# Paged attention on one core: block transposes on VectorE and transfers within SBUF in place of TensorE transposes

## The chip, the cores and the metric

One core of a Trainium2 chip runs the whole kernel. The metric is device time in microseconds (us) of one execution. Less is better.

## The reference, cut to what matters

The input x has 64 sequences of 32 tokens of 512 numbers. First each sequence is multiplied by a small matrix chosen by its condition and added to itself. Then follows attention over a paged cache of keys and values with new keys appended. All of it is float32.

```python
x = x + einsum('bct,bcd->bdt', x, weights[condition])
q = einsum('bsd,ed->bse', x, Wq).reshape(64, 32, 32, 128)     # 32 query heads
k = einsum('bsd,ed->bse', x, Wk).reshape(64, 32, 8, 128)      # 8 key heads
v = einsum('bsd,ed->bse', x, Wv).reshape(64, 32, 8, 128)
q, k = rope(rmsnorm(q, q_norm_w), pos), rope(rmsnorm(k, k_norm_w), pos)
k_all = concat([k_cache[block_table] (512 rows), k]); v_all likewise
scores = einsum('bqhd,bkhd->bhqk', q, repeat(k_all, 4)) * SCALE   # 4 query heads share a key head
probs = softmax(where(valid, scores, -1e30))
o = einsum('bhqk,bkhd->bqhd', probs, repeat(v_all, 4))
out = x + einsum('bse,de->bsd', o.reshape(64, 32, 4096), Wo)
```

## The kernel before, in words

A **step** handles 4 sequences (128 tokens, one per partition) and 4 of the 8 key heads with their 16 query heads. There are 32 steps: 16 groups of sequences for the first half of the heads (`hh` 0), then the same 16 for the second half (`hh` 1). The output of the first half waits in DRAM in `acc_d`, and the transposed input of a group in `x1t_d`.

Each step is cut into 16 **slots**, one for each sequence (`bt`) and key head (`g`); slot = 4 bt + g. A slot always has the scores of one head against 512 cached keys (`ps`, L534), the exponential on ScalarE (`pr`, L542) and the product of probabilities and values of the slot before (`po`, L592). Around these, the loop issues by a table the preparation of the *next* step, called `ahead`:

- `x1_c` (`pmix`, L353) and `x1_b` (`px1t`, L361) mix and transpose the input, in slots 2 and 3, for steps of the first half only;
- `k_a` and `q_a` project (`pp`, L397: 8 TensorE instructions with 512 columns), then `norm_rope` normalises and rotates on ScalarE, VectorE and GpSimd: `sq` L407, `ms` L411 and L412, `rs` L414, `rope` and `ropeu` L418, L425, L431, L433;
- `k_b` and `q_b` transpose the 128x128 result of each of four heads on TensorE (`pt`, L441) and copy it out of PSUM on ScalarE (L454, L469). There are five such groups of four in a step, in slots 6, 8, 10 and 13;
- `v_a` projects the new values.

`out_proj` of the step *before* (`pout`, L481, 32 TensorE instructions) stands whole in slot 3. The scores against new keys (`psn`, L552) are in slot 0, their values (`pnv`, L576, copied out at L584) in slots 1 and 3. `psn`, `pnv`, `pp`, `pt`, `pmix`, `px1t` and `pout` share a ring of four PSUM tiles.

The keys of a sequence come as 16 transfers of 64 KB from the SP queue (`k_t`, L286), issued in the first slot of a sequence for the sequence after the next one. They land in one of two buffers, and VectorE copies them head by head into one of four `kh` tiles (L527). Values come by indirect transfers from GpSimd (`raw`, L310, three buffers) and are masked by ScalarE (`v`, L323). `turn` (L617) is a VectorE transpose in 32x32 blocks, used here for the attention output alone. TensorE's and SP's instructions run in the order in which the program writes them; the order on the other engines is a scheduler's.

Of the kernel before, what the change touches and what calls it, by code (L numbers as in the profile page):

```python
# [19 lines left out]
P = 128  # L20
# [35 lines left out]
def cond_resid_paged_attention_kernel(  # L56
# [67 lines left out]
    rden = const.tile([P, NHH * NT * BT, GH], F32, tag="rden", name="rden")  # L124
# [61 lines left out]
    def steps_of(exact, pools):  # L186
# [31 lines left out]

        last = {}
# [44 lines left out]

        def load_x(t):
            xt = work.tile([P, HID], F32, tag="acc", name=f"xt_{t}_{uid}", bufs=3)
            nc.sync.dma_start(xt, x[t * P : (t + 1) * P, :])
            return xt
# [62 lines left out]
        class Step:  # L331
            def __init__(self, n):
                self.n, self.hh, self.t = n, n // NT, n % NT
                self.name = f"{n}_{uid}"
                self.qt = {}

        def x1_a(st):

            nonlocal x_next
            t = st.t  # L340
            if st.hh:
                st.acc = work.tile([P, HID], F32, tag="acc", name=f"acc_{st.name}", bufs=3)
                nc.sync.dma_start(st.acc, acc_d[t])
                st.x1t = work.tile([P, KC, P], F32, tag="x1t", name=f"x1t_{st.name}", bufs=1)
                nc.sync.dma_start(st.x1t.rearrange("p c q -> p (c q)"), x1t_d[t])
                return
            st.acc = x_next
# [54 lines left out]
        def norm_rope(st, pp, name, kind):  # L402

            cw, sw = st.rot[kind]
            p4 = pp.rearrange("p (h e f) -> p h e f", h=4, e=2)
            sq = work.tile([P, 4, D], F32, tag="w2", name=f"sq_{name}", bufs=1)
            nc.scalar.activation(  # L407
                sq.rearrange("p h d -> p (h d)"), pp, AF.Square, scale=1.0 / math.sqrt(D)
            )
            ms = small.tile([P, 4], F32, tag="ms", name=f"ms_{name}")  # L410
            nc.vector.tensor_reduce(ms, sq, AX.X, ALU.add)  # L411
            nc.vector.tensor_scalar_add(ms, ms, EPS)  # L412
            rs = small.tile([P, 4], F32, tag="rs", name=f"rs_{name}")
            nc.gpsimd.tensor_tensor(rs, ms, minus_half, ALU.pow)  # L414

            r = work.tile([P, 4, 2, HD], F32, tag="w1", name=f"rope_{name}")
            u = work.tile([P, 4, 2, HD], F32, tag="w2", name=f"ropeu_{name}", bufs=1)
            nc.vector.tensor_tensor(  # L418
                r.rearrange("p h e f -> p h (e f)"),
                pp.rearrange("p (h d) -> p h d", h=4),  # L420
                cw.rearrange("p e f -> p (e f)").unsqueeze(1).to_broadcast([P, 4, D]),
                ALU.mult,
            )
            for e in range(2):
                nc.vector.tensor_tensor(  # L425
                    u[:, :, e, :],
                    p4[:, :, 1 - e, :],
                    sw[:, e, :].unsqueeze(1).to_broadcast([P, 4, HD]),
                    ALU.mult,
                )  # L430
            nc.vector.tensor_tensor(r, r, u, ALU.add)  # L431
            rd = r.rearrange("p h e f -> p h (e f)")
            nc.vector.tensor_tensor(  # L433
                rd, rd, rs.unsqueeze(2).to_broadcast([P, 4, D]), ALU.mult
            )
            return rd
# [6 lines left out]

        def k_a(st):
            if st.n > 1 or exact:
                rot_tables(st)
            name = f"k_{st.name}"
            pp = project(st, wt["k", st.hh, 0], f"pp_{name}")
            st.k_rope = norm_rope(st, pp, name, "k")

        def k_b(st):
            pt = transposed(st.k_rope, f"k_{st.name}")
            st.kn = act.tile([P, GH, P], F32, tag="kn", name=f"kn_{st.name}")
            nc.scalar.copy(st.kn, pt)  # L454
# [6 lines left out]
        def q_a(st, g):  # L461
            name = f"q_{st.name}_{g}"
            pp = project(st, wt["q", st.hh, g], f"pp_{name}")
            st.qt[g] = norm_rope(st, pp, name, "q")

        def q_b(st, g):
            pt = transposed(st.qt[g], f"q_{st.name}_{g}")
            qt = act.tile([P, BT, REP, S], F32, tag=f"qt{g}", name=f"qt_{st.name}_{g}")
            nc.scalar.copy(  # L469
                qt.rearrange("p b h s -> p h b s"),  # L470
                pt.rearrange("p h (b s) -> p h b s", b=BT),
            )
            st.qt[g] = qt

        def out_proj(st, halfway=None):

            po = ps_p.tile([P, HID], F32, tag="pp", name=f"pout_{st.name}")
            for i in range(QH):
                if halfway and i == 3 * QH // 4:
                    halfway()  # L480
                nc.tensor.matmul(  # L481
                    po,
# [5 lines left out]
            nc.vector.tensor_tensor(st.acc, po, st.acc, ALU.add)  # L488
            if exact or st is steps[-1]:
                store(st)  # L490
# [27 lines left out]
        def queries(ba, g):  # L518
            return ba.st.qt[g][:, ba.bt].rearrange("p h s -> p (h s)")
# [25 lines left out]
        def new_scores(st):  # L545
# [3 lines left out]
            for g in range(GH):  # L549
                for bt in range(BT):  # L550
# [3 lines left out]
                        st.kn[:, g, own],  # L554
                        st.qt[g][:, bt].rearrange("p h s -> p (h s)"),
# [30 lines left out]
        def values(ba, g):  # L586
# [12 lines left out]
            if g == 0:  # L599
                ba.o = work.tile([P, GH, D], F32, tag="o", name=f"o_{ba.name}", bufs=1)  # L600
            if g % 2:
# [3 lines left out]
                rd = rden[:, ba.n, both]  # L605
# [17 lines left out]
        def exact_batch(ba, key_no):  # L623
# [7 lines left out]
            for g in range(GH):  # L631
# [9 lines left out]
                    st.kn[:, g, bt * S : (bt + 1) * S],  # L641
# [43 lines left out]
        x_next = load_x(0)  # L685
        if exact:
# [7 lines left out]
            for st in steps:  # L694
# [6 lines left out]
                if st.n:  # L701
                    x_next = st.hh or load_x(st.t)
                if not st.hh:
                    load_cond_weights(st.t)
                x1_a(st)
                x1_c(st)
                x1_b(st)
                k_a(st)
# [8 lines left out]
                out_proj(st)  # L717
# [3 lines left out]
        first, second = steps[0:2]  # L721
        load_w("q", 0, 0)
# [15 lines left out]
        x_second = load_x(1)  # L738
# [14 lines left out]
        trig = work.tile([P, 3, TRIG * HD], F32, tag="w1", name="trig0")  # L753
# [4 lines left out]
        x1_a(first)  # L758
        x1_c(first)
        x_next = x_second  # L760
# [8 lines left out]
        trig = work.tile([P, 3, TRIG * HD], F32, tag="w1", name="trig1")  # L769
# [21 lines left out]
        x1_a(second)  # L791
# [30 lines left out]
        def pieces(st):  # L822
            do = {
                0: (x1_a,),
                4: (k_a, (q_a, 0)),
                5: ((q_a, 1),),
                6: (v_a, k_b, (q_b, 0)),
                8: ((q_a, 2), (q_b, 1)),
                10: ((q_a, 3), (q_b, 2)),
                13: ((q_b, 3),),  # L830
            }
            if st is second:
                do[4], do[6] = ((q_a, 0),), (k_b, (q_b, 0))
            return do

        valued, turned = (batch, GH - 1), batch
# [13 lines left out]
        x_next = load_x(2)  # L850
        load_cond_weights(2)
        for st in steps:
            if st.n:
                new_ot(st)
            ahead = steps[st.n + 1] if st.n + 1 < len(steps) else None
            fill = pieces(ahead) if ahead else {}
            for bt in range(0 if st.n else 1, BT):
# [5 lines left out]
                for g in range(GH):  # L863
# [14 lines left out]
                    if slot == 2 and ahead:  # L878
                        x1_c(ahead)
                    if slot == 3:  # L880
                        if ahead:
                            x1_b(ahead)
                        out_proj(steps[st.n - 1])
                        if st.n + 1 < NT // TRIG:
                            tmp = work.tile([P, 3, TRIG * HD], F32, tag="w1", name=f"trig_{st.n}")
                            with tc.issue_after(last["dve"]), tc.issue_after(last["act"]):
                                angles((st.n + 1) * TRIG, tmp)
                    if slot == 5 and st.n:
                        store(steps[st.n - 1])
                    if slot == 6 and 0 < st.n and st.n + 2 < NT:  # L890
                        x_next = load_x(st.n + 2)
                        load_cond_weights(st.n + 2)
                    if st.t == 0:
                        load_parts([("o", i) for i in range(GH)], st.hh, slot - GH)
                    if st.n in (NT - 2, NT - 1):
                        load_parts(
                            [("k", 0), ("q", 0), ("q", 1), ("v", 0), ("q", 2), ("q", 3)],
# [3 lines left out]
                    if unfilled and (slot == GH - 1 or bt and g or unfilled[0][0] is this):  # L901
                        for _ in range(1 if bt or g == 0 else VC):
# [4 lines left out]
                    if g == 1 and turned is not None:  # L907
                        turn(turned)
                    if later is not None:
                        head_keys(later, g)  # L910
                turned = this
                batch, later = later, after
        turn(turned, slice(0, 2))
        values(*valued)
        turn(turned, slice(2, GH))


        def in_range():
            rd = rden.rearrange("p n g -> p (n g)")
            good = work.tile([P, NHH * NT * BT * GH], F32, tag="w1", name="good")  # L920
            nc.vector.tensor_scalar(good, rd, DEN_LOW, None, ALU.is_ge)
            nc.vector.scalar_tensor_tensor(good, rd, DEN_HIGH, good, ALU.is_le, ALU.mult)
            count = small.tile([P, 1], F32, tag="ms", name="count")
            nc.vector.tensor_reduce(count, good, AX.X, ALU.add)
            ones = small.tile([P, 1], F32, tag="rs", name="ones")
            nc.vector.memset(ones, 1.0)
            pc = ps_p.tile([1, 1], F32, tag="pp", name="pcount")
            nc.tensor.matmul(pc, count, ones, start=True, stop=True)
# [4 lines left out]
        out_proj(steps[-1], in_range)  # L933
# [57 lines left out]
```

## Time and profile before

| | |
|---|---|
| median of 3 runs | 2262.68 us (2262.07 to 2267.07) |
| the profiled execution's own time | 2258.59 us |
| its span in the profile | 2256.8 us |
| VectorE busy | 1076.0 us (48%) |
| ScalarE busy | 940.4 us (42%) |
| GpSimd busy | 779.8 us (35%) |
| transfers | 318.13 MB, 141 GB/s in the mean |

A busy share is an average over the whole span. TensorE instructions are pipelined, so the sum of their durations is more than the time that they take; the distance from one group's start to the next one's start tells what a group costs.

### The profile page before, as it was taken

To read this page: it belongs to the slowest core of one execution; us is meant where nothing else is said; L and a number is where in the kernel's file an instruction comes from. 1 tells how busy PE (TensorE), PEld (TensorE's weight loads), DVE (VectorE), ACT (ScalarE), POOL (GpSimd) and SP (SyncE) were. 2 spreads that over 40 slices of the span, in tenths; PEclk is the share of its full clock that TensorE was granted. 3 is DMA by queue.
4 is the path that set the end of the run, shared out by engine and by line. 5 is a ranking of instruction groups with operands and counts; after the bars stand their busy time and mean duration, and the time that the engine had idled before them with its cause. 6 is when DMAs were issued, how large, how long until landed. Compare 5 with 4: busy or idle time off the path is not lost.

```text
span 2256.8 us, 41920 instructions
## 1 busy us (share of the span) xinstructions
PE 2223.5 (99%) x13590; PEld 1565.7 (69%) x13590; DVE 1076.0 (48%) x2722; ACT 940.4 (42%) x1724; POOL 779.8 (35%) x1008
## 2 busy tenths in 40 slices
PE   8999999999999999999999999999999999999998
PEld 5767677676776677766777666777666777666775
DVE  5545455443554444543545544455444455444452
ACT  3534454444433444433444333443334443343442
POOL 4423333233433333332333333333323343233331
PEclk9999999999999999999999999999999999999999
DMA  7744544345443455435756444553344544444542
GB/s 229 195 131 128 154 134 128 114 128 154 142 121 113 130 152 155 116 113 157 229 168 169 124 137 138 154 148 115 115 145 139 160 124 127 124 130 151 159 116 74
DMA packets 364053, 318.13 MB, mean 141 GB/s; under 512 B 46800, under 2 KB 308960, under 8 KB 363824
## 3 DMA queue, kind: packets, MB, share of 16 engines
q1 hardware_dynamic: 319104, 174.44, 27.0%
q0 software_dynamic: 41712, 136.66, 20.4%
q10 hardware_dynamic: 3008, 4.25, 0.5%
q8 instruction: 110, 1.80, 0.3%
q14 instruction: 119, 0.97, 0.1%
HBM read 302.59 MB, written 12.58 MB: 140 GB/s over the span
## 4 chain that ended last, share of the span: by engine, by line
PE 90%; DMA 4%; DVE 2%; issue 2%; SPq 2%; ACT 1%; POOL 1%; ACTq 0%; DVEq 0%; POOLq 0%
PE pout_x L481 19%; PE pp_q_x L397 19%; PE po_x L592 18%; PE ps_x L534 18%; PE pp_k_x L397 5%; PE pp_v_x L397 5%; PE pt_q_x L441 2%; PE pnv_x L576 2%; DMA raw_x<-in_vc_dram,v_row 2%; SPq L286 1%; PE psn_x L552 1%; DMA k_t_x<-in_kt_dram 1%; PE pt_k_x L441 1%; PE pmix_x L353 1%; DMA pages_at<-in_pages_v_dram 0%
## 5 line engine op out<-in xcount | busy, mean ns | idle before, releaser
L310 POOL DMA_INDIRECT raw_x<-in_vc_dram,v_row x512 | 515.0, 1006 | 718.6 <-ACT v_x L323 659.3
L542 ACT ACTIVATE pr_x<-ps_x 128x512 f32<-128x512 f32 x512 | 305.4, 600 | 628.3 <-PE ps_x L534 624.8
L592 PE MATMUL po_x<-v_x,pr_x 128*128 128x129 f32 x4096 | 551.9, 278 | 5.6 <-ACT pr_x L542 5.6
L534 PE MATMUL ps_x<-qt_x,kh_x 128*128 128x128 f32 x4096 | 542.1, 275 | 2.8 <-DVE kh_x L527 2.2
L592 PEld LDWEIGHTS po_x<-v_x,pr_x 128*128 128x128 f32 x4096 | 503.1, 192 | 49.5 <-issue 30.4
L534 PEld LDWEIGHTS ps_x<-qt_x,kh_x 128*128 128x128 f32 x4096 | 502.8, 192 | 27.3 <-issue 19.8
L397 PE MATMUL pp_q_x<-wq_x,x1t_x 128*128 128x512 f32 x1024 | 463.7, 596 | 3.3 <-ACT qt_x L469 3.3
L481 PE MATMUL pout_x<-wo_x,ot_x 128*128 128x512 f32 x1024 | 445.0, 592 | 0.0
L323 ACT ACTIVATE v_x<-raw_x,valid 128x512 f32<-128x512 f32 x512 | 362.6, 724 | 114.4 <-DMA raw_x<-in_vc_dram,v_row 113.9
L481 PEld LDWEIGHTS pout_x<-wo_x,ot_x 128*128 128x128 f32 x1024 | 192.2, 190 | 229.0 <-issue 228.7
L397 PEld LDWEIGHTS pp_q_x<-wq_x,x1t_x 128*128 128x128 f32 x1024 | 188.4, 192 | 203.8 <-issue 200.1
L527 DVE COPY kh_x<-k_t_x 128x512 f32<-128x512 f32 x506 | 213.2, 424 | 108.8 <-DMA k_t_x<-in_kt_dram 68.2
L407 ACT ACTIVATE sq_q_x<-pp_q_x 128x512 f32<-128x512 f32 x128 | 76.4, 597 | 306.5 <-issue 135.4
L411 DVE TENSOR_REDUCE ms_q_x<-sq_q_x 128x4 f32<-128x512 f32 x128 | 87.4, 682 | 200.0 <-ACT sq_q_x L407 200.0
L414 POOL TENSOR_TENSOR rs_q_x<-ms_q_x,minus_half 128x4 f32<-128x4 f32 x128 | 132.9, 1038 | 132.7 <-DVE ms_q_x L412 132.7
L604 DVE TENSOR_TENSOR nv_x<-po_x,nv_x 128x258 f32<-128x258 f32 x256 | 107.7, 421 | 146.9 <-PE po_x L592 138.7
L386 POOL TENSOR_TENSOR cw_k_x<-norm_k,cos 128x64 f32<-128x64 f32 x32 | 10.1, 315 | 382.7 <-DVE ms_k_x L412 382.7
L418 DVE TENSOR_TENSOR rope_q_x<-pp_q_x,cw_q_x 128x512 f32<-128x512 f32 x128 | 87.3, 682 | 103.4 <-PE pt_k_x L441 103.4
L488 DVE TENSOR_TENSOR xt_x<-pout_x,xt_x 128x512 f32<-128x512 f32 x16 | 11.1, 692 | 246.6 <-PE pout_x L481 246.6
L488 DVE TENSOR_TENSOR acc_x<-pout_x,acc_x 128x512 f32<-128x512 f32 x16 | 11.1, 692 | 220.7 <-PE pout_x L481 220.7
L397 PE MATMUL pp_v_x<-wv_x,x1t_x 128*128 128x512 f32 x256 | 115.2, 593 | 0.0
L397 PE MATMUL pp_k_x<-wk_x,x1t_x 128*128 128x512 f32 x256 | 115.2, 593 | 0.0
(99 smaller groups left out, 1575.7 us busy)
## 6 DMA issues: line engine op xcount, KB each, us to landing
k_t_x<-in_kt_dram SPq DMA_DIRECT2D x2048, 64.0 KB
raw_x<-in_vc_dram,v_row POOLq DMA_INDIRECT x512, 4.0
wo_x<-in_wo_dram SPq DMA_DIRECT2D x32, 256.0 KB
xt_x<-in_x_dram SPq DMA_DIRECT2D x16, 256.0 KB
x1t_d<-x1t_x ACTq DMA_DIRECT2D x16, 256.0 KB
acc_d<-xt_x SPq DMA_DIRECT2D x16, 256.0 KB
wq_x<-in_wq_dram SPq DMA_DIRECT2D x8, 512.0 KB
acc_x<-acc_d SPq DMA_DIRECT2D x16, 256.0 KB
```

Of the source, the lines that this page charges most:

```text
L310: nc.gpsimd.indirect_dma_start(out=raw.rearrange("p g d -> p (g d)"), out_offset=None, in_=vc, in_offset=bass.IndirectOffsetOnAxis(ap=v_ro ...
L323: nc.scalar.activation(v_bufs[b % 2][:, c, :, 0:D], raw, AF.Copy, scale=ok)
L397: nc.tensor.matmul(pp, st.x1t[:, c, :], w[:, c, :], start=(c == 0), stop=(c == KC - 1))
L411: nc.vector.tensor_reduce(ms, sq, AX.X, ALU.add)
L414: nc.gpsimd.tensor_tensor(rs, ms, minus_half, ALU.pow)
L418: nc.vector.tensor_tensor(r.rearrange("p h e f -> p h (e f)"), pp.rearrange("p (h d) -> p h d", h=4), cw.rearrange("p e f -> p (e f)").uns ...
L481: nc.tensor.matmul(po, st.ot[:, i, :], wt["o", st.hh, i // 4][:, i % 4, :], start=(i == 0), stop=(i == QH - 1),)
L527: last["dve"] = nc.vector.tensor_copy(k, ba.k_raw[:, :, g, :]).ins
L534: nc.tensor.matmul(ps[:, c, :], ba.k[g][:, c * P : (c + 1) * P], queries(ba, g), start=True, stop=True,)
L542: last["act"] = nc.scalar.activation(pr, ps, AF.Exp, scale=SCALE).ins
L592: nc.tensor.matmul(ba.po[:, g % 2, :], ba.pr[g][:, c, :], ba.v_t[:, c, g, :], start=(c == 0), stop=(c == VC - 1),)
L604: nc.vector.tensor_tensor(t, ba.po, t, ALU.add)
```

## The change

Queries and new keys of all steps but the first are no longer transposed by TensorE. VectorE transposes each rotated 128x512 tile in 32x32 blocks into `rows` (`turn_rows`). That puts each block of 32 features on the partitions of its own sequence. Sixteen transfers within SBUF, of 32 partitions x 2560 bytes (80 KB) each, then carry the blocks to the partitions where the products want them (`spread`). The first step keeps the TensorE way, with its copy out of PSUM now in two pieces. The columns of sequences 0 to 2 lie in one buffer (`q_cols`), those of sequence 3 in one of two (`q_last`).

The order within a step changes: the input of a step is loaded, mixed and transposed during the step two before it, the five projections stand in slots 3 to 7, the two halves of `out_proj` in slots 8 and 9, and `v_a` in slot 13. Fills of the value buffers are spread evenly over the slots, and the check on denominators is counted in two halves.

```diff
+        rows = wpool.tile([P, 4, GH + 1, P], F32, tag="rows", ...)
+        q_cols = wpool.tile([P, BT - 1, GH + 1, P], F32, tag="q_cols", ...)
+        q_last = [wpool.tile([P, GH + 1, P], F32, ...) for i in range(2)]
...
+        def turn_rows(st, i, rd, name):
+            nc.vector.transpose(
+                rows[:, :, i, :].rearrange("p k (h s) -> p h k s", h=4),
+                rd.rearrange("p h (k d) -> p h k d", k=4),
+            )
+        def columns(st, bt):
+            return q_last[st.n % 2] if bt == BT - 1 else q_cols[:, bt]
+        def spread(st, batches):
+            for bt in batches:
+                for k in range(4):
+                    nc.sync.dma_start(
+                        columns(st, bt)[k * S : (k + 1) * S, :, :],
+                        rows[bt * S : (bt + 1) * S, k, :, :],
+                    )
+        def by_tensor(st):
+            return st.n == 0 or exact
+        def finish(st, i, pp, name, kind):
+            if by_tensor(st):
+                norm_rope(st, pp, name, kind, rows[:, :, i, :])
+            else:
+                turn_rows(st, i, norm_rope(st, pp, name, kind), name)
...
         def pieces(st):
             do = {
-                0: (x1_a,),
-                4: (k_a, (q_a, 0)),
+                2: (rot_tables,),
+                3: (k_a,),
+                4: ((q_a, 0),),
                 5: ((q_a, 1),),
-                6: (v_a, k_b, (q_b, 0)),
-                8: ((q_a, 2), (q_b, 1)),
-                10: ((q_a, 3), (q_b, 2)),
-                13: ((q_b, 3),),
+                6: ((q_a, 2),),
+                7: ((q_a, 3),),
+                9: ((spread, (0, 1, 3)),),
+                11: ((spread, (2,)),),
+                13: (v_a,),
             }
...
-                    if slot == 2 and ahead:
-                        x1_c(ahead)
-                    if slot == 3:
-                        if ahead:
-                            x1_b(ahead)
-                        out_proj(steps[st.n - 1])
+                    if slot in (8, 9) and st.n:
+                        out_proj(steps[st.n - 1], slice((slot - 8) * QH // 2, (slot - 7) * QH // 2))
+                    if slot == 9:
+                        if st.n:
+                            new_ot(st)
+                        for ba in turned:
+                            turn(ba)
...
-                    if slot == 5 and st.n:
+                    if slot == 10 and st.n:
                         store(steps[st.n - 1])
+                    if st.n and beyond:
+                        if slot == 6 and not beyond.hh:
+                            load_cond_weights(beyond.t)
+                        if slot == 11:
+                            x1_a(beyond)
+                    if slot == 13 and beyond:
+                        x1_t(beyond)
+                    if slot == 14 and beyond:
+                        x1_c(beyond)
+                    if slot == 15 and beyond:
+                        x1_b(beyond)
...
-                    if unfilled and (slot == GH - 1 or bt and g or unfilled[0][0] is this):
-                        for _ in range(1 if bt or g == 0 else VC):
+                    for _ in range({1: 0, GH: 2}.get(slot, 1)):
+                        if unfilled and (g or unfilled[0][0] is this):
                             next_values()
```

## The prediction

> **What bounds the kernel now.** I read the engine table first, then the chain of work that ended last.
>
> ```profile
> PE 2223.5 (99%) x13590; PEld 1565.7 (69%) x13590; DVE 1076.0 (48%) x2722; ACT 940.4 (42%) x1724; POOL 779.8 (35%) x1008
> ...
> PE 90%; DMA 4%; DVE 2%; issue 2%; SPq 2%; ACT 1%; POOL 1%; ACTq 0%; DVEq 0%; POOLq 0%
> PE pout_x L481 19%; PE pp_q_x L397 19%; PE po_x L592 18%; PE ps_x L534 18%; PE pp_k_x L397 5%; PE pp_v_x L397 5%; PE pt_q_x L441 2%; PE pnv_x L576 2%; DMA raw_x<-in_vc_dram,v_row 2%; SPq L286 1%; PE psn_x L552 1%; DMA k_t_x<-in_kt_dram 1%;
> ```
>
> TensorE (PE) carries the chain, and the change takes work from it: `pt` is 2% for the queries, and the keys' share falls below the rows shown. For the cost of one group I take the distance of starts in the same chain in order of time (start, length, what):
>
> ```profile
> 1059.77 3.44 PE pp_v_x L397 x8
> 1063.20 0.44 PE pt_k_x L441 x4
> 1063.64 0.44 PE pt_q_x L441 x4
> 1064.08 0.89 PE po_x L592 x8
> 1064.97 0.89 PE ps_x L534 x8
> ```
>
> Four transposes cost 0.44 us (1063.64 - 1063.20), with no gap around them. `psn` starts every 68.02 us in an undisturbed step of the second half and 69.47 us in one of the first half (which adds `pmix`, 0.96, and `px1t`, 0.44). The sum of all steps' excess over these two floors, step 2 onwards, is 26 us: PE waits little. One of the longer waits, in order of time:
>
> ```profile
> 381.49 0.54 DVE kh_x L527
> 382.05 0.33 SPq L286
> ...
> 382.57 0.33 SPq L286
> ...
> 389.26 0.33 SPq L286
> ...
> 389.78 4.67 DMA k_t_x<-in_kt_dram
> ```
>
> Here a key copy freed a buffer, SP issued transfers 0.515 us apart, and the last landed 4.67 us later. In the order before, sequence 3 of a step (slots 12 to 15) has only 7.6 us of PE work (8 groups of 0.89 and one `pt`), less than the 9.3 us that SP needs for one sequence's keys (16 x 0.515 and a page read of 1.0). So keys and values run late around the end of a step.
>
> **What the Trainium skill says.** "VectorE: DVE Perf Modes", The three transpose paths: VectorE transposes only within 32x32 blocks, from SBUF to SBUF, so the blocks must still be moved across partitions. The trace agrees as far as it goes: `ot` is made in such blocks, 709 ns for 128x512. "DMA: Bandwidth & Descriptors", Anatomy of one DMA: about 2.0 us fixed plus bytes / 436e3. For 80 KB that is an estimate of 2.2 us per transfer; the key transfers, 64 KB each, show landings of 1.7 to 4.7 us in the chain, so I use 5 us. "Perfetto Trace Analysis", Transposes: TensorE's transposes skip arithmetic. The trace agrees: 0.44 us against 0.89 us for four float32 products of the same size.
>
> **The change part by part.**
>
> *PE transposes leave.* Five groups in each of steps 1 to 31: 155 x 0.4375 = **-67.8 us**, all on the path.
>
> *`pmix` no longer sits between the two `pnv`.* Behind it, `pnv` needed the PSUM tile that VectorE had still to empty:
>
> ```profile
> 1026.64 1.13 PE pmix_x L353 x2
> 1027.76 0.89 PE ps_x L534 x8
> 1028.65 1.09 PE pnv_x L576 x16
> ```
>
> It costs 0.66 where no `pmix` precedes: 15 x 0.43 = **-6.5 us**. In its new place, slot 14, `px1t` follows 1.8 us after `pmix` (a `po` and a `ps` lie between), and needs the VectorE add of 0.69 done: no cost if VectorE is free, as it is in these slots, up to 1 us x 14 if not.
>
> *VectorE gains* 155 transposes of 709 ns (the `ot` row): +110 us, 1076 to about 1186 of some 2180, 54%. The tight place is slots 3 to 7, where five projections stand in a row. By distances of starts, one projection takes VectorE 0.60 + 0.08 + 0.60 + 0.66 + 0.60 + 0.69 = 3.2 us, the new transpose 0.6 to 0.7, a `kh` copy 0.33, half of a `nv`, `rden`, `o` group 0.4: 4.7 us, against 2 x 0.89 + 3.44 = 5.22 us of PE. It fits by 0.5. Should the four-level pattern make the transpose take twice as long, 0.2 a slot are missing, 1 us after five slots; the `kh` copies behind it have four slots of room and slots 8 and 9 (8.66 us each) catch up. Cost 0; if the cover is gone, the first late thing is `nv`, for which `po` waits.
>
> *ScalarE loses* the PSUM copies of 155 groups, 0.587 each (L454, L469): -91 us, off the path. In slots 15 to 3 it has 5 exponentials, 4 masks, 8 `nv` copies, `pn` and `x1t`: 3.0 + 2.9 + 3.2 + 0.6 + 0.6 = 10.3 us against 11.7 us of PE, so 0 here too, though with little room.
>
> *SP and the queues gain* 16 transfers a step. An issue is 0.33 us, 0.515 with the register work that the keys need: 5.3 to 8.3 us a step on top of some 37, out of 66. Bytes: 31 x 16 x 80 KB = 40.6 MB more than 318, about 164 GB/s in the mean; slices of the page reach 229. Twelve are issued in slot 9, behind the keys of slot 8 and the last `rows` tile; PE needs them in slot 16, over 20 us later. The tight ones are the four of sequence 2, which may not overwrite `q_cols` before the scores of slot 11. From there PE has `po`, slots 12 to 15 and one `ps`: 11.6 us in the second half, 13 in the first, until `psn` reads them. Issue 4 x 0.33 to 0.515 and 5 us for the landing are 6.3 to 7.1 us. So they are hidden, with 4.5 us or more to spare. Behind them on SP stand the new input (`x1_a`, wanted by `pmix` 9 us later) and the keys of slot 12, late by about 2.5 us; those are copied from slot 0 on and used in slot 4. `x1_t` in slot 13 waits for `v_a` of the same slot; the next keys behind it belong to slot 0. I put 0, with 0 to +10 us.
>
> *The order.* Sequence 3 now has 10.7 to 12 us of PE instead of 7.6, sequence 0 about 13, sequences 1 and 2 about 21 each. Both ends now exceed the 9.3 us of SP, and no more than three short slots with fills follow each other. Of the 26 us of excess, and about 12 in the first and last steps, I take **-6 us**; the bounds are -30 and +15, since the weights' change of half (steps 14 and 15) and the last step, whose slots 0 to 7 are now all short, could be worse. The opening copies five tiles in two pieces: **+1 us**.
>
> Sum: -67.8 - 6.5 - 6 + 1 = -79.3. The profiled execution took 2258.59 us (2256.8 span and 1.8 around it), 4.1 below the median 2262.68. So 2179.3 for that execution and 2183.4 for the median: **2184 us**, 3.5% less.
>
> **The rivals.**
>
> 1. *The transposes leave, but waits give back a part* (0.20). VectorE with five projections in a row, or values fetched later because the queues carry 13% more. For it: ScalarE's 1.4 us of room in slots 15 to 3. Against: waits at PE are small now, in an order with a shorter sequence 3. At 0.6 to 1.6 us a step, 19 to 50 of the 79 return: 2203 to 2234 us.
>
> 2. *The spread is late and PE waits for it at `psn` in each step* (0.09): slower. Place: the four transfers of sequence 2, between slot 11 and slot 0. Price: the wait itself, on PE, 31 times. It decides from 79 / 31 = 2.6 us a step, so when issue and landing together take over 14 us instead of 7: for example if these transfers, 32 partitions wide, ran at a third of the speed of the key transfers, and those of slot 9 were still under way. With 5 us a step the time would be 2184 + 155 = 2339. Against it: 80 KB is little more than one key transfer, and none of those in the chain took over 4.7 us.
>
> 3. *PE's work is replaced by nothing on the path and by nothing off it* (0.03): the groups of 0.44 us would have to hide a wait that appears once they are gone, for instance for key transfers limited by SP. SP waits 663 us for key copies, so it is not full; 2258 to 2267.
>
> **How the numbers follow.** Main case 0.68 (2164 to 2203), rival 1 0.20, rival 2 0.09, rival 3 0.03. The range 2164 to 2230 holds the main case and most of rival 1. 0.2% of the time, 4.5 us, is about what a measurement tells from no change: faster 0.88, same 0.03, slower 0.09.
>
> **What the next profile would show.** Right: `pt` groups only at the start; STREAM_TRANSPOSE of 128x512 282 times (127 + 155) at about 0.7 us; PE busy near 2150; `psn` every 66 to 67 us (68.02 - 2.19, and 69.47 - 2.19 - 0.43). VectorE near 1186, ScalarE near 850; 41 MB more on SP's queue; no PE wait on a transfer from `rows`. Wrong: PE rows for `psn` or `ps` with a releaser of `q_cols` or `q_last`, of over 1 us in most steps (rival 2); `po` or `pp` waiting for VectorE or ScalarE in slots 3 to 9 (rival 1); step lengths still at 68 with PE idle elsewhere (rival 3).

## The result, and the profile after

The changed kernel takes 2201.69 us (median of 4, 2201.13 to 2204.06) against 2262.63 (median of 4): ratio 0.9728, 95% interval 0.9712 to 0.9745, so 2.7% less. The forecast was 2184 us and 3.5%. 61 us came, 79 were expected. The profiled execution took 2204.06 us with a span of 2202.3.

First the engine table and the chain that ended last, from the page of the kernel after:

```profile
PE 2156.6 (98%) x12970; PEld 1502.4 (68%) x12970; DVE 1198.1 (54%) x2881; ACT 867.5 (39%) x1574; POOL 806.1 (37%) x1008
...
PE 93%; DMA 3%; SPq 2%; issue 1%; ACT 1%; DVE 0%; POOL 0%; DVEq 0%; ACTq 0%; POOLq 0%
```

TensorE still bounds. The groups of operations, each shape apart, show what took over from it (after the bar: busy us, then mean ns of one):

```profile
L451 DVE STREAM_TRANSPOSE rows_x<-rope_q_x 128x512 f32<-128x512 f32 x124 | 87.6, 707 | 2.1
L451 DVE STREAM_TRANSPOSE rows_x<-rope_k_x 128x512 f32<-128x512 f32 x31 | 22.0, 711 | 1.0
L445 PE MATMUL pt_x<-ident,rows_x 128*128 128x128 f32 x20 | 3.0, 273 | 0.0
```

155 block transposes at 0.71 us, as priced, and TensorE transposes queries and keys in the first step alone (20 instructions, five groups). The end of an undisturbed step, in the chain in order of time (start, length, what):

```profile
860.32 0.86 PE pmix_x L357 x2
861.18 0.89 PE po_x L628 x8
862.07 0.89 PE ps_x L570 x8
862.96 0.44 PE px1t_x L365 x4
863.40 0.89 PE po_x L628 x8
864.29 0.89 PE ps_x L570 x8
865.19 1.01 PE psn_x L588 x32
866.20 1.09 PE po_x L628 x8
867.29 0.89 PE ps_x L570 x8
868.18 0.66 PE pnv_x L612 x16
```

There is no gap. `pmix` and `px1t` wait for nothing, `pnv` takes its short 0.66 us, and `psn` reads the spread columns without a pause. Steps take 67.1 us in the first half and 65.9 in the second, where 67 (66.85) and 65.8 were forecast. So the missing 18 us are not in the ordinary step. They are in two others, as the starts of `psn` show (a step runs from one start to the next; us, profiled executions; the last three columns are experiments told below):

| | before | after | order alone | weights later | and second step on TensorE |
|---|---|---|---|---|---|
| to the first `psn` | 56.7 | 58.3 | 56.3 | 55.4 | 57.2 |
| step 0 | 46.6 | 44.9 | 47.4 | 46.4 | 47.8 |
| **step 1** | 75.5 | **90.6** | 76.1 | 82.9 | 71.6 |
| steps 2 to 13 | 840.9 | 805.6 | 831.8 | 805.5 | 805.5 |
| steps 14 to 16 | 209.2 | 197.9 | 204.1 | 197.5 | 198.1 |
| **step 17** | 70.8 | **77.7** | 75.1 | 65.8 | 65.8 |
| steps 18 to 30 | 888.7 | 856.6 | 884.2 | 857.1 | 856.7 |
| step 31 and end | 68.5 | 70.7 | 68.6 | 68.9 | 68.8 |
| span | 2256.8 | 2202.3 | 2243.5 | 2179.5 | 2171.6 |

The first row is not read further: with an opening that is the same as in the kernel after, two experiments told below (turn_twice and spread_14) have 54.4 and 55.1 there.

What TensorE waits for in the kernel after (us in total, times, longest):

```profile
PE ps_x L570 <- DVE kh_x L563: 13.7, 4, 4.8
PE psn_x L588 <- DMA q_cols_x<-rows_x: 8.8, 1, 8.8
...
PE pp_k_x L401 <- DMA x1t_x<-x1t_d: 3.0, 1, 3.0
```

One wait for the spread, of 8.8 us, at the start of step 1; none in the thirty others. The `kh` waits are in steps 1 and 17 too, three of the four of them; `x1t` is in step 17. SP's issues show how late that spread was (start, time from the first of them to the end of the last, line, how many):

```profile
93.09 4.85 SPq L465 DMA_DIRECT2D q_cols_x<-rows_x  x8
97.99 4.07 SPq L465 DMA_DIRECT2D q_last_x<-rows_x  x4
102.10 1.07 SPq L249 DMA_DIRECT2D wo_x<-in_wo_dram  x2
103.27 3.07 SPq L465 DMA_DIRECT2D q_cols_x<-rows_x  x4
```

`psn` began at 103.18, so the twelve had 10.1 us and the last four came too late. In an ordinary step, whose `psn` begins at 865.19, they have 26.5 and 13.6 us:

```profile
838.64 4.97 SPq L465 DMA_DIRECT2D q_cols_x<-rows_x  x8
...
851.55 2.41 SPq L465 DMA_DIRECT2D q_cols_x<-rows_x  x4
```

What stands before the waits is told by the chain around the start of step 1 (its longest pieces):

```profile
97.22 6.27 DMA raw_x<-in_vc_dram,v_row
103.56 7.02 DMA x1t_d<-x1t_x
...
123.00 6.34 DMA wo_x<-in_wo_dram
```

and around the start of step 17:

```profile
1201.73 0.44 SPq L249
...
1202.21 0.50 SPq L249
...
1202.81 7.13 DMA x1t_x<-x1t_d
...
1210.08 5.17 PE pp_k_x L401 x8
```

L249 issues the output weights of the new half, `wo`. In these two places they stand on SP's queue between the spread, the input and the keys, and the transfers behind them land late: `x1t` takes 7.13 us. Issues are held up too. The transfers of SP's and ScalarE's queues share eight semaphores in this program, and an issue waits until the transfer that had its semaphore before, as a rule the eighth before it, has landed. So the weight issue at 110.61 waited for `x1t_d` in the chain above, and key issues waited for weights:

```profile
SPq L291 <- DMA wo_x<-in_wo_dram: 15.9, 17, 2.0
```

The changed order had moved them there, from slots 4 to 11 of a half's first step to slots 10 to 15 and 0 to 1.

### The profile page after: what moved, and what is told of

The parts are those of the page before. It is cut to its first block, busy times and chain, and to the rows that moved or that the text cites. A ratio compares the mean times of both kernels' runs of the same rounds, so it can differ in the third digit from the quotient of the medians.

```text
span 2202.3 us, 41557 instructions
## 1 busy us (share of the span) xinstructions
PE 2156.6 (98%) x12970; PEld 1502.4 (68%) x12970; DVE 1198.1 (54%) x2881; ACT 867.5 (39%) x1574; POOL 806.1 (37%) x1008
## 4 chain that ended last, share of the span: by engine, by line
PE 93%; DMA 3%; SPq 2%; issue 1%; ACT 1%; DVE 0%; POOL 0%; DVEq 0%; ACTq 0%; POOLq 0%
PE po_x L628 20%; PE pout_x L516 20%; PE ps_x L570 20%; PE pp_q_x L401 19%; PE pp_k_x L401 5%; PE pp_v_x L401 5%; PE pnv_x L612 2%; PE psn_x L588 1%; SPq L291 1%; DMA k_t_x<-in_kt_dram 1%; PE pmix_x L357 1%; DMA raw_x<-in_vc_dram,v_row 0%; DMA x1t_d<-x1t_x 0%; DMA x1t_x<-x1t_d 0%; DMA wq_x<-in_wq_dram 0%
## 5 line engine op out<-in xcount | busy, mean ns | idle before, releaser
L315 POOL DMA_INDIRECT raw_x<-in_vc_dram,v_row x512 | 538.8, 1052 | 837.9 <-ACT v_x L328 769.3
L628 PEld LDWEIGHTS po_x<-v_x,pr_x 128*128 128x128 f32 x4096 | 516.5, 192 | 125.5 <-issue 114.8
L570 PE MATMUL ps_x<-q_cols_x,kh_x 128*128 128x128 f32 x3072 | 408.7, 276 | 14.2 <-DVE kh_x L563 13.7
L570 PEld LDWEIGHTS ps_x<-q_cols_x,kh_x 128*128 128x128 f32 x3072 | 378.7, 193 | 31.9 <-issue 26.4
L328 ACT ACTIVATE v_x<-raw_x,valid 128x512 f32<-128x512 f32 x512 | 363.0, 716 | 11.6 <-DMA raw_x<-in_vc_dram,v_row 11.2
L563 DVE COPY kh_x<-k_t_x 128x512 f32<-128x512 f32 x506 | 205.2, 417 | 181.4 <-PE ps_x L570 151.2
L418 POOL TENSOR_TENSOR rs_q_x<-ms_q_x,minus_half 128x4 f32<-128x4 f32 x128 | 140.4, 1097 | 176.3 <-DVE ms_q_x L416 176.3
L570 PE MATMUL ps_x<-q_last_x,kh_x 128*128 128x128 f32 x1024 | 135.3, 275 | 0.0
L524 DVE TENSOR_TENSOR acc_x<-pout_x,acc_x 128x512 f32<-128x512 f32 x32 | 22.1, 692 | 200.2 <-PE pout_x L516 200.2
L570 PEld LDWEIGHTS ps_x<-q_last_x,kh_x 128*128 128x128 f32 x1024 | 124.6, 192 | 0.0
L415 DVE TENSOR_REDUCE ms_q_x<-sq_q_x 128x4 f32<-128x512 f32 x128 | 86.5, 676 | 54.4 <-ACT sq_q_x L411 52.7
L649 DVE TENSOR_TENSOR o_x<-nv_x,rden 128x256 f32<-128x256 f32 x256 | 108.5, 424 | 6.5
```

What stands on the lines that cost most here:

```text
L315: nc.gpsimd.indirect_dma_start(out=raw.rearrange("p g d -> p (g d)"), out_offset=None, in_=vc, in_offset=bass.IndirectOffsetOnAxis(ap=v_ro ...
L328: nc.scalar.activation(v_bufs[b % 2][:, c, :, 0:D], raw, AF.Copy, scale=ok)
L563: last["dve"] = nc.vector.tensor_copy(k, ba.k_raw[:, :, g, :]).ins
L570: nc.tensor.matmul(ps[:, c, :], ba.k[g][:, c * P : (c + 1) * P], queries(ba, g), start=True, stop=True,)
L628: nc.tensor.matmul(ba.po[:, g % 2, :], ba.pr[g][:, c, :], ba.v_t[:, c, g, :], start=(c == 0), stop=(c == VC - 1),)
L649: nc.vector.tensor_tensor(ba.o[:, both, :], t[:, :, 0:D], rd.unsqueeze(2).to_broadcast([P, 2, D]), ALU.mult,)
```

## The experiments

The theory (A) was: the ordinary step keeps the whole gain, and the loss comes from the weights' place and from the first step, in which no output projection covers the spread. The rivals were bandwidth at that place, an order worth much by itself, a VectorE at its limit, and a spread with more room than reckoned. Each chip ran the kernel before as well; the ratios are to that.

**The weights later** (label wo_late).

```diff
-                    if st.t < 2:
-                        load_parts([("o", i) for i in range(GH)], st.hh, slot - 10 + st.t * BT * GH)
+                    if st.t == 1:
+                        load_parts([("o", i) for i in range(GH)], st.hh, slot)
```

> The changed kernel with one edit: the output weights of a half are loaded in slots 0 to 7 of the half's second step, one part a slot, instead of slots 10 to 15 of its first step and 0 and 1 of its second. Theory A (the changed kernel loses its time in two places, step 1 at 90.6 us and step 17 at 77.7 us, because 16 weight transfers stand on SP between the spread and the keys there): step 17 comes down to 66 to 68 us, step 1 to 72 to 82 us (the first step still has no output projection to cover its spread), all other steps stay at 67.1 and 65.9; 2172 to 2186 us. Rival B (the weights must be moved at some time, 4 MB beside 4 MB of keys and values, and the two places are limited by bandwidth): the loss moves to slots 4 to 8 of the same steps, within 5 us of 2201.7.

Measured: 2182.44 us (2181.32 to 2186.65) on a chip where the kernel before takes 2259.01; ratio 0.9668, interval 0.9655 to 0.9681, against 0.9728 for the kernel after. Step 17 falls from 77.7 to 65.8: its whole excess was the weights' place, and there the bandwidth rival falls. Step 1 falls to 82.9 only, just above the range. In it TensorE waits once more for the spread, and part of the loss has moved to later slots, as that rival had said ("issue" as a releaser means that the profile shows none):

```profile
PE pmix_x L357 <- issue: 4.3, 1, 4.3
PE psn_x L588 <- DMA q_cols_x<-rows_x: 4.0, 1, 4.0
...
PE pout_x L516 <- issue: 2.5, 2, 1.5
```

SP issued the last two weight transfers at 149.9 and 151.9, each held by an earlier one, and TensorE stood before `pout` at 150.9 and 155.6. The input for `pmix` was issued at 174.7, behind the next spread, and `pmix` started at 177.5. So SP is still behind in this step.

**The second step on TensorE as well** (late_second): the edit above, with nothing spread in the first step.

```diff
         def by_tensor(st):
-            return st.n == 0 or exact
+            return st.n < 2 or exact
...
             if st is second:
-                do[2] = do[3] = do[13] = ()
+                do[2] = do[3] = do[9] = do[11] = ()
+                do[12], do[13] = (k_b, (q_b, 0)), ((q_b, 1),)
+                do[14], do[15] = ((q_b, 2),), ((q_b, 3),)
```

> The run with the output weights in slots 0 to 7 (from SP), and the second step's queries and keys transposed by TensorE too, in slots 12 to 15 of the first step, so that nothing is spread in the first step, which has no output projection to cover it. Theory A: five groups cost 2.2 us, the wait of 4 us for the spread and its lower clock go, and SP is free of 16 issues at 0.6 us (10 us) before the weights: step 1 falls from 82.9 to 70 to 76 us; 2172 to 2180. If the keys and weights of step 1 alone are more than SP can issue, step 1 stays over 80 and the time rises by 2 us.

Measured: 2173.51 us (2167.90 to 2176.89), the kernel before 2261.74; ratio 0.9609, interval 0.9588 to 0.9630. Step 1 takes 71.6, with one wait of TensorE, 2.7 us before `pmix`. SP issues the same keys and weights there as in the run before, so these alone are not more than it can issue. That the missing output projection made the spread late is reckoned from its 13.7 us; no run puts one into the first step. This version beats both kernels: 3.9% less than before, and its interval lies below that of the kernel after.

**The weights on ScalarE's queue** (wo_act): the first edit, with these transfers issued by `nc.scalar` in place of `nc.sync`.

> The run with the output weights in slots 0 to 7 of a half's second step, with these 16 transfers issued by ScalarE's queue instead of SP's. If SP's issue time is what makes step 1 long (82.9 us there, against 67.1 for its neighbours), 16 x 0.47 = 7.5 us leave SP and step 1 falls to 74 to 79 us: 2172 to 2179 on a chip where that run takes 2182. If it is the transfers' landing (a key transfer waits until the eighth transfer before it has landed, whichever queue issued it) or the first step's short cover for its spread, step 1 stays within 3 us of 82.9.

Measured: 2189.04 us (2187.19 to 2189.88), ratio 0.9675 (0.9657 to 0.9692), no better than from SP. Step 1 does fall to 72.5, even below the range, but this does not tell SP's issue time from the transfers' landing. ScalarE's queue is ordered by the scheduler, which had put the first half's loads, free of dependencies, into the opening: all 16 were issued between 2.9 and 83.4 us, and step 1 begins at 119.5. So it was rid of both at once. In return the first `psn` comes at 72.7 us instead of 55.4, and ScalarE's instructions wait there for `wo` transfers (7.4 us in one place). That is more than the 10 us saved in step 1.

**The order alone** (tensor_turn): all steps transposed by TensorE, nothing spread.

```diff
-            return st.n == 0 or exact
+            return True
...
-                9: ((spread, (0, 1, 3)),),
-                11: ((spread, (2,)),),
-                13: (v_a,),
+                12: (k_b, (q_b, 0)),
+                13: (v_a, (q_b, 1)),
+                14: ((q_b, 2),),
+                15: ((q_b, 3),),
...
```

> The changed kernel with the transposes of all steps on TensorE again, in slots 12 to 15 of its new order; no block transposes of queries and keys and no spread. Theory A (a group of four transposes costs its 0.44 us on TensorE and nothing else is bound to it): steps of the second half take 65.9 + 2.2 = 68.1 us, of the first 69.3; step 1 loses its wait for the spread (9 us); 2201.7 + 68 - 9 = 2261 us, the time of the kernel before within 0.4%. Rival C (the new order is worth much by itself): under 2245 us. Rival D (ten more copies out of PSUM in four short slots make ScalarE late): over 2280 us, with waits for its copies.

Measured: 2247.36 us (2245.33 to 2248.54), ratio 0.9952 (0.9936 to 0.9967). So the order by itself gives 0.5%, 11.6 us, and ScalarE is not late. The time lies between theory A's 2261, which had left the order's own share out, and the 2245 of rival C; neither foretold it. Steps of the two halves take 69.3 and 68.0, as it said: against the kernel after they differ by 26.2 / 12 = 2.18 us (steps 2 to 13) and 27.6 / 13 = 2.12 (18 to 30), the five groups of 0.44. Step 17 takes 75.1 here without any spread, which leaves the weights as its cause. Step 1 takes 76.1 where the kernel after takes 90.6: there the spread is needed for the loss. With wo_act, step 1 can be set out by cause, as excess over an ordinary step: 5.4 us with the spread and no weights near it (72.5 - 67.1), 6.8 with the weights and no spread (76.1 - 69.3), 23.5 with both (90.6 - 67.1). Together they cost 11 us more than their sum. Each figure is from one profiled execution, and wo_act has another opening too.

**The block transposes twice** (turn_twice): the `nc.vector.transpose` of `turn_rows` is written twice.

> The changed kernel with each of the 155 block transposes of queries and keys done twice. By theory A VectorE has the room: it takes 0.6 to 0.7 us more in each of slots 3 to 7, some 1 us of lateness after five slots, caught up in slots 8 and 9: 2201.7, within 4 us. Rival E (VectorE is nearly the bound in slots 3 to 7, and its lateness reaches TensorE by po or by the spread): 0.7 us x 155 = 108 us at most, so up to 2310 us; 1 us a step would give 2233.

Measured: 2204.49 us, ratio 0.9761 (0.9747 to 0.9776). VectorE is busy 1295.7 us instead of 1198.1, and steps 2 to 13 take 805.5 us as before the doubling. Another 0.7 us in each of five slots in a row costs the ordinary step nothing. Steps 1 and 17 grow by 2.2 us each (to 92.8 and 79.9). Over the whole run SP waits 232.7 us for VectorE's key copies instead of 218.8, which would fit; the cause is not shown.

**The last four transfers later** (spread_14): `spread` of sequence 2 goes from slot 11 to slot 14, behind the keys of slot 12.

> The changed kernel with all sixteen spread transfers moved: those of sequences 0, 1 and 3 stay in slot 9 and those of sequence 2 go from slot 11 to slot 14, behind the keys that SP issues from slot 12 on. It measures the room that the prediction gave to the last four transfers (4.5 us or more). Theory A: they now start 9 us later, when 4 us are left until the new keys' scores; issue 2.5 us and landing 3 to 5 us make TensorE wait 1.5 to 3.5 us in each of 30 steps: 2245 to 2305 us. Rival F (a transfer's landing is short, or SP is not there in time anyway and the order of slots 11 and 12 matters little): within 10 us of 2201.7.

Measured, one run: 2328.11 us, slower than the kernel before and somewhat over the range. Waits of TensorE:

```profile
PE psn_x L588 <- DMA q_cols_x<-rows_x: 120.5, 30, 24.4
```

and one of them in the chain in order of time:

```profile
1023.90 0.91 PE po_x L628 x8
...
1026.14 3.45 DMA q_cols_x<-rows_x
1029.64 1.07 PE psn_x L588 x28
```

This is rival 2 of the prediction, made by hand. The thirty waits are uneven: three take 24.4, 12.9 and 9.7 us, and the middle one 3.1. The room that slot 11 leaves is read from the kernel after: in steps 2 to 31 the last packet of 2560 bytes ends 2.0 to 3.9 us after the last issue, and `psn` starts 5.9 to 8.8 us later still, more than the 4.5 that the prediction asked for.

**The projections in their old slots** (old_slots), with the transposes and spread kept.

```diff
-                3: (k_a,),
-                4: ((q_a, 0),),
-                5: ((q_a, 1),),
-                6: ((q_a, 2),),
-                7: ((q_a, 3),),
-                9: ((spread, (0, 1, 3)),),
-                11: ((spread, (2,)),),
-                13: (v_a,),
+                4: (k_a, (q_a, 0)),
+                5: ((q_a, 1),),
+                6: (v_a,),
+                8: ((q_a, 2),),
+                10: ((q_a, 3),),
+                11: ((spread, (0, 1, 3)), (spread, (2,))),
...
-                    if slot in (8, 9) and st.n:
-                        out_proj(steps[st.n - 1], slice((slot - 8) * QH // 2, (slot - 7) * QH // 2))
+                    if slot == 3 and st.n:
+                        out_proj(steps[st.n - 1], slice(0, QH))
```

> The changed kernel with the block transposes and the spread kept, but the projections back in slots 4 (keys and queries 0), 5, 8 and 10, new values in slot 6, the whole output projection in slot 3 and all sixteen spread transfers in slot 11. It tells whether the transposes can be had without the order. Theory A: the last rotated tile is ready some 4 us after slot 10, then SP issues 16 transfers at 0.62 us (10 us) and they land 3 us later, 17 us in all, where TensorE has some 12 us left before the new keys' scores: 5 us of waiting in each of 30 steps, and a lower clock after each wait as in the run with the late spread; 2330 to 2430 us, slower than the kernel before. Rival G (the two-step-ahead input and the even fills are what the transposes need, the place of the projections is not): under 2230 us.

Measured, one run: 2601.6 us, most steps 74 to 86. TensorE waits in each step, and most of it not where the theory had put it:

```profile
PE pmix_x L357 <- DMA acc_x<-in_x_dram: 115.5, 9, 14.2
PE psn_x L588 <- DMA q_cols_x<-rows_x: 77.5, 31, 5.6
```

The new input stands behind the spread on SP's queue, and `pmix` wants it in slot 14, before `psn`. The time is far from rival G's. But the edit moved the projections, the output projection and twelve spread transfers together, and left the input behind them; the old slots with the input issued ahead of the spread were not tried.

## Why the prediction was right or wrong

The time lies inside the range, and by 1.3 us inside that of the main case (2164 to 2203). The mechanism was right in the ordinary step. That the number held is in part luck: steps 1 and 17 grew by 22.0 us, for which the sum had nothing, and the ordinary steps (2 to 16 and 18 to 30) gained 78.7 us, which it had expected of all steps together.

- **TensorE's transposes, -67.8 us:** right. 2.12 to 2.18 us a step, against 2.19. The lines in the prediction show the price, not the reason given from the Trainium skill: a float32 product stands there as two records (`po` has 8 for four products), and each takes as long as one record of a transpose, 0.11 us (0.89 / 8 and 0.44 / 4). That a transpose skips arithmetic ("Perfetto Trace Analysis", Transposes) is shown by no run here.
- **`pnv` without `pmix` before it, -6.5:** right in kind, more in size. By distances of starts the 64 groups take 42.9 us instead of 52.7, so -9.8. `px1t` does not wait behind `pmix`.
- **VectorE and ScalarE, 0:** right, and shown for VectorE by the doubling. For ScalarE it is read from the waits: TensorE waits for it five times in the kernel after, 2.6 us in all.
- **The order, with the opening and `pnv`, -11.5 in all:** the order alone gives -11.6. This agreement hides two errors: the ordinary steps gained more than reckoned, and step 17 lost 4.3 us even without the spread. The excess of 26 us from which the -6 was taken does not come out of the starts of `psn`: steps 2 to 30 stand 18 us above the two floors, and 24 with step 1.
- **The spread, 0 to +10:** right in thirty steps, wrong in one. An issue takes 0.583 us in the middle and 0.63 from start to start, not 0.33 to 0.515, so sixteen take SP 10 us; the landing was short, 2.0 to 3.9 us to the last packet and not 5. The estimate of 2.2 us is near that, but the fit behind it is given in the Trainium skill ("DMA: Bandwidth & Descriptors", Anatomy of one DMA) for transfers that GpSimd issues, and these are SP's. The step that failed is the sentence that twelve transfers have "over 20 us" and four have 11.6. In the first step no output projection stands in slots 8 and 9, and 13.7 us of that cover are absent; two weight transfers stood between the twelve and the four as well. The twelve had 10.1 us, SP was not done, and TensorE waited 8.8 us, of which 4.0 stayed when the weights were moved away.
- **A move left out.** The list of moves did not count the 16 weight transfers that the same edit took to other slots. The bound of +15 under *The order* named steps 14 and 15, with the projections' weights, and the last step; steps 14 and 15 became shorter and the last step with the end grew by 2.2 us, while steps 1 and 17 grew by 22.0 together (15.1 and 6.9).
- **Rival 1** was near in outcome: a part was given back, some 18 us, just short of its 19 to 50. Its mechanism did not occur: neither VectorE nor the values' fetches, and not in each step. Rivals 2 and 3 did not occur; spread_14 shows what rival 2 costs.

The loss of step 1 is not a sum of two shares: spread and weights cost little alone there and 11 us more when they meet. Both go through SP's queue and its eight semaphores; how much of it is issue time and how much landing is not separated.

## What to carry to other kernels

Work that leaves the bounding engine is worth its distance of starts, if the transfers that take its place have their cover in every step: reckon the first step and the step after a change of weights apart, since the average step says nothing on them. List every issue that an edit moves on an in-order queue, also those of other data that it moves along. A load without dependencies on a scheduled queue may be put far earlier than it is written: here, for a step that begins at 119.5 us, from 2.9 us on.

## What the runs showed of the hardware

A long wait of TensorE can cost more than its length. In step 1 of the kernel after, TensorE waits 16.7 us (8.8 for the spread, 7.9 for keys), and the step is 23.5 us longer than its neighbours. The windows of the kernel after (TensorE's busy time first; the column behind the counts is the granted clock):

```profile
100.00:135.00 35.00, 23.16 (x171) 17.88 (x170) 9.70 (x25) 12.14 (x24) 8.82 (x12) 0.80 0.86 201
700.00:767.00 67.00, 67.00 (x407) 46.70 (x406) 37.04 (x89) 26.39 (x48) 25.00 (x32) 1.00 0.56 159
```

After the waits of step 1 the clock was 0.80 in the mean of 35 us, and the `pp_k` after the wait in step 17 took 5.17 us instead of 3.44. Over the whole span it was 0.997 before, 0.991 after, 0.975 with the late spread and 0.925 with the old slots. With the late spread the waiting itself is the larger part: its span is 124 us longer than that of the kernel after (2326.3 and 2202.3), and TensorE's busy time, for the same instructions, 31.5 us longer (2188.1 and 2156.6).

The Trainium skill, "TensorE: Matmul & The Clock Gate", What's actually happening, says that TensorE falls to half its clock after an idle window of about 3.4 us. The trace agrees on half the clock and on stretches of 3.4 us or multiples of it: 0.80 over 35 us is some 14 us at half the clock, about four such stretches. The length of a wait does not decide it here. In the kernel after, a stretch of half the clock began 2.1 us into a wait of 2.82 us; with the late spread one followed a wait of 2.02 us, and none a wait of 3.15 us. So a wait shorter than 3.4 us can be enough, and a few waits in two steps weigh on the result.
